# Biases as rows spread by TensorE, earlier loads, and an order from a table, in an attention and FP4 feed-forward kernel

## The chip, the cores and the metric

The kernel runs on one core of a Trainium2 chip. The core has five engines that run side by side, each with its own queue of instructions, worked off in order: TensorE (PE in the profile; its weight loads are PEld), VectorE (DVE), ScalarE (ACT), GpSimd (POOL) and SyncE (SP, which here only asks for transfers). Transfers (DMAs) are also asked for by ACT. An instruction that needs another engine's result waits at the head of its queue, and all behind it waits too.

The metric is the device time of one launch in microseconds (us). Before the change three runs gave 790.79, 791.53 and 792.86, median 791.53.

## What is computed

x has 16 batches of 512 tokens of 256 elements, in fp32. Cut to what matters:

```python
# attention, 16 heads of 16
q, k, v = x @ Wq + bq, x @ Wk + bk, x @ Wv + bv
p = exp(t - max(t))                      # per head, for t = q and t = k
q, k = p / (sum(p) + 1e-6)
attn = (q @ k.T) / (sum(q) + 1e-6)       # no softmax: it is linear
x = layernorm(x + (attn @ v) @ Wo + bo)

# feed-forward, 256 -> 704 -> 256
def fp4_linear(x, w):                    # blocks of 16 rounded to FP4 with a scale
    return fp4_quant_dequant(x) @ fp4_quant_dequant(w).T
h = silu(fp4_linear(x, w_gate)) * fp4_linear(x, w_up)
x = layernorm(x + fp4_linear(h, w_down))
```

## The kernel before

**Stages.** A batch is four tiles of 128 tokens, or two pairs of tiles; there are 32 pairs. Per batch, `project` transposes x on PE (L636) into a PSUM bank, ACT copies it out (L639), PE multiplies by Wq and Wk (L778, 128x512), DVE adds the biases (L781) and takes the maxima (L786), POOL subtracts them (L790). `features` takes exp on ACT (L801), sums, reciprocals on DVE (L803 to L814) and the scaling on POOL (L820). `key_values` sums the keys (L829), multiplies keys by x (L836), goes through Wv with its bias (L852, L853) and Wo (L864), with the copies L843, L857 and L870 between, which gives one matrix M per batch. `attend` transposes q (L636), multiplies by M (L892), adds x and b_o (from L885) and normalises (`norm`, L718 to L755), and writes the result to DRAM.

The feed-forward runs per pair. `quantise` reads the pair back (L910), rounds it to codes (`codes`, L655 to L668), and regroups the codes through DRAM (`regroup`: one write g, then four reads, L676 and L681) and the scales too (`spread_scales`: four small writes d, L699, one spreading read, L704); POOL multiplies both into xqT (L929). `gate_up` does 32 passes of PE per pair (L957; an fp32 matmul is two passes in the trace), silu and product (L962, L964), and codes, regrouping (g_h, hcT, d_h) and L1009 on POOL make hq. `down` multiplies hq by the down weights, 24 passes (L1026), normalises and writes y (L1038, asked for by ACT). The last pair, which nothing follows, transposes on PE (L977 to L995). Once, early on, the weights are rounded (`weight_scales` L509 to L534, `fp4_exact` L563 to L584) and transposed (L597, L620).

**Loads.** `load_all` asks for x of batch 0 in two halves, then on ACT's queue for Wq, Wk, Wv and on SP's for the three biases, each spread over 128 partitions by its transfer (128x256, L462). `load_x` of batch 1 asks for x and then, by `load_rest`, for w_o, b_o (spread in the same way, L466), the gate and up weights in four pieces and the down weights. x of batches 2 and 3 follows.

**What sets the order.** The code records every operation with `Plan.op(eng, us, due, fn, ins, outs, ...)`: an estimated cost in us and a due value. `Plan.order` then lists them: it goes through modelled time, always takes what can start first, and among operations of an engine that can start within 0.02 us of each other the one with the lowest due. The list fixes each engine's queue (`tc.manual_schedule`). Nothing is reordered on the chip. `LAG` is the modelled delay from an engine to another, `t_pe`, `t_dve`, `t_act`, `t_pool` give costs by size, and a transfer counts with an assumed landing time:

```python
            t, o = min(((t, o) for t, o in c if t <= first + 0.02), key=lambda x: (x[1].due, x[1].at))
```

**PSUM** has seven shared banks (tags pt, pg, pm with least and most numbers) and one that holds small tiles. Transfers go round eight semaphores: one that is issued waits for the one eight issues earlier.

Of the kernel before, what the change touches and what calls it, by code (L numbers as in the profile page):

```python
# [17 lines left out]
P = 128  # L18
# [4 lines left out]

FIRST = 2
# [3 lines left out]
LAG = 0.3  # L28
# [16 lines left out]
UNTIE = 1.0 + 2.0**-17  # L45

# [45 lines left out]
class Op:  # L92
    __slots__ = ("eng", "us", "fn", "due", "preds", "succs", "left", "bufs", "new", "start", "end", "table", "port", "name", "at")


class Plan:
# [47 lines left out]
    def order(self):  # L144
# [32 lines left out]
        def start(o, at):  # L177
            if o.port:
                at = max(at, port)
            for p in o.preds:  # L180
                at = max(at, p.end + (LAG if p.eng != o.eng else 0.0))
# [20 lines left out]
        while len(out) < len(self.ops):  # L202
# [17 lines left out]
            free[o.eng] = o.end  # L220
# [12 lines left out]
            for b in o.bufs:  # L233
                left, end = ends.get(id(b), (b.users, 0.0))
                ends[id(b)] = left - 1, max(end, o.end)
# [10 lines left out]
def t_pe(n):  # L246
    return 2 * (n / 1200.0 + 0.002)


def t_dve(n):  # L250
    return 0.15 + n / 960.0


def t_act(n):
    return 0.16 + n / 1200.0


def t_ts(n):
    return 0.15 + n / 1920.0


def t_pool(n):
    return 0.07 + n / 525.0
# [3 lines left out]
def tile_favor_fp4_block(  # L267
# [63 lines left out]
    def psum(tag, name):  # L331
        return Bank(share, tag, name)
# [57 lines left out]
    def load_x(b, due):  # L390
        x = buf([TPB, D], "x", 4, f"x_{b}")
        rows = hidden[b].rearrange("(t p) d -> p t d", p=P)
        if b:
            op("SP", 0.1, due, lambda: nc.sync.dma_start(x.tile, rows), outs=[x])
            op(f"DMA:x{b}" if b < 4 else "DMA", (0, 9.0, 16.0, 18.0, 3.5)[min(b, 4)], due, lambda: None, outs=[x])
        else:

            def halves():
                for p in range(PPB):
                    nc.sync.dma_start(x[:, 2 * p : 2 * p + 2, :], rows[:, 2 * p : 2 * p + 2, :])  # L400

            op("SP", 0.1, due, halves, outs=[x])
            for p in range(PPB):
                op(f"DMA:x{b}{p}", 4.5 + p, due, lambda: None, outs=[(x, p)])
        if b == 1:
            op("SP", 0.1, due, load_rest)
        xs[b] = x

    w_qkv = const.tile([P, DC, D3], F32, name="w_qkv")
    b_qkv = const.tile([P, D3], F32, name="b_qkv")  # L410
    w_o = const.tile([P, DC, D], F32, name="w_o")
    b_o = const.tile([P, D], F32, name="b_o")
# [32 lines left out]
    wqkv_in, wo_in = (loaded(n, t) for n, t in (("wqkv", 7.0), ("wo", 14.0)))  # L445
    NGU, NDN = NW * D // F2, DC * FF // F2
    op("DMA:wgu", 16.0, 0.0, lambda: None, outs=[(gu_b, k) for k in range(NGU)])
    op("DMA:wdn", 20.0, 0.0, lambda: None, outs=[(dn_b, k) for k in range(NDN)])
# [3 lines left out]
    def load_all():  # L452

        head = [o for o in plan.ops if o.eng == "SP"][:1]
        for o in head:
            for b in o.new:
                b.make()
            o.fn()
            o.fn = lambda: None
        for i, (w, bias) in enumerate(((Wq, bq), (Wk, bk), (Wv, bv))):  # L460
            nc.scalar.dma_start(w_qkv[:, :, i * D : (i + 1) * D], w.rearrange("(c p) n -> p c n", p=P))
            nc.sync.dma_start(b_qkv[:, i * D : (i + 1) * D], bias.partition_broadcast(P))  # L462

    def load_rest():
        nc.sync.dma_start(w_o, Wo.rearrange("(c p) n -> p c n", p=P))
        nc.sync.dma_start(b_o, bo.partition_broadcast(P))  # L466
        gu_b.make()
        dn_b.make()
        gu_raw, dn_raw = gu_rows(), dn_rows()
        for i, w in enumerate((w_gate, w_up)):  # L470
# [3 lines left out]
            nc.sync.dma_start(gu_raw[i * TR : (i + 1) * TR, 2 * NR, :], w[NR * P :])  # L474
        nc.sync.dma_start(dn_raw, w_down.rearrange("(c p) k -> p c k", p=P))

    def fill():
        make_identity(nc, ident)
        nc.gpsimd.memset(neg_half, -0.5)
# [17 lines left out]
    def weight_scales(src, src_b, n, at, name, due):  # L497
# [38 lines left out]
        op("DVE", 11 * fast + 0.0063 * nb, due, rest, ins=[pb], outs=[sc_b, *iv])  # L536
        return part, sc_b, iv

    def fp4_exact(src, src_b, scales, sc_b, iv, k, name, due):
# [14 lines left out]
        d, g, a = t_dve(F2), t_pool(F2), t_act(F2)  # L554
# [27 lines left out]
        op("DVE", t_ts(F2), due, lambda: nc.vector.tensor_scalar(c(), lower(y()), 6, None, ALU.logical_shift_left),  # L582
# [59 lines left out]
    def codes(src, xn, sq, dst, key, n, scales, at, name, due, sat=None):  # L642
# [19 lines left out]
        op("DVE", 0.27 + 0.0073 * nb, due, scale, ins=[(amax, key)], outs=[(nscale, key), (inv, key)])  # L662
# [9 lines left out]
    def regroup(src, dst, n, tag, name, due):  # L672
# [3 lines left out]
        dma(f"g{name}", 3.0, due, lambda: nc.sync.dma_start(d.tile, src.tile), ins=[src], outs=[d])  # L676
# [6 lines left out]
        dma(f"h{name}", 3.5, due, back, ins=[d], outs=[dst], issue=1.8)  # L683

    def spread_scales(nscale, G, dst, tag, name, due, holds=()):
# [8 lines left out]
        ), ins=[nscale], outs=[sT], port=True)  # L694
# [6 lines left out]
        dma(f"w{name}", 4.0, due, write, ins=[sT], outs=[d], issue=1.8)  # L701
        into, dst_b = dst

        dma(f"r{name}", 3.0 + 0.7 * G, due, lambda: nc.sync.dma_start(  # L704
# [3 lines left out]
    def norm(pr, add, dst, name, due, ins, r, junk, us=range(2)):  # L708
# [3 lines left out]
        if n == 1:  # L712
# [10 lines left out]
            op("DVE", 2 * t_dve(D) + 0.1, due, stats, ins=[(pr, key)] + ins, outs=[(r, key), st, mv])  # L723
            op("POOL", 0.7, due, lambda: nc.gpsimd.tensor_tensor(rstd.tile, mv[:, 1:2], neg_half[:, :1], ALU.pow), ins=[mv], outs=[rstd])
# [12 lines left out]
        op("DVE", n * (t_dve(D) + 0.06), due, total, ins=[(pr, key)] + ins, outs=[(r, key), rs])  # L737
# [12 lines left out]
        op("ACT", 0.35 + 0.6 * n, due, square, ins=[(r, key), rs], outs=[(dst, key), var, nm])  # L750
        op("POOL", 1.1, due, root, ins=[nm], outs=[var, rstd, nb])
# [366 lines left out]
```

## Time and profile before

| what | value |
|---|---|
| runs, median | 791.53 us |
| profiled execution, span | 792.0 us |
| PE busy | 768.6 us (97%) |
| DVE busy | 656.7 us (83%) |
| POOL busy | 455.9 us (58%) |
| ACT busy | 416.5 us (53%) |
| weights' last piece landed | 18.9 us |
| last PE pass ends | 786.8 us |

The page's chain that ended last, followed back from the last instruction, gives by engine, in shares of the span:

```profile
PE 62%; DVE 12%; DMA 8%; POOL 8%; issue 4%; ACT 4%; SPq 2%; ACTq 0%; POOLq 0%; DVEq 0%
```

Busy time counts an instruction from its start to its end. PE's passes overlap, so a pass's busy time (0.27 to 0.6 us) is more than the distance from one to the next.

### The profile page before, as it was taken

Reading aid. Unit: us, or ns where it says so; the run is one execution under the profiler, and the core shown is the slowest. Engines: PE = TensorE matmul, PEld = TensorE weight load, DVE = VectorE, ACT = ScalarE, POOL = GpSimd, SP = SyncE. Lnnn points to the kernel's source line nnn. Section 1 sums busy time; section 2 is a strip of 40 time slices with the busy share of each in tenths; the row PEclk is TensorE's granted clock in tenths of the full one; section 3 lists DMA queues with packets and bytes.
Section 4 is the critical chain, followed back from the end, with each engine's and each line's share of the span. In section 5 each row is a group of like instructions: output and inputs, shape, how many; then the busy total and the mean of one; then the engine's idle time right before and its main releaser. Section 6 shows DMA issues by size and latency. Waiting matters only on the chain.

```text
span 792.0 us, 10915 instructions
## 1 busy us (share of the span) xinstructions
PE 768.6 (97%) x3118; PEld 552.5 (70%) x3118; DVE 656.7 (83%) x1340; ACT 416.5 (53%) x893; POOL 455.9 (58%) x602
## 2 busy tenths in 40 slices
PE   7999999989998999999999999999999999999996
PEld 3567657657676777767777777777777777777774
DVE  2998999999888798697697798888878988778784
ACT  2347766868887783544545444444334444344441
POOL 5668788889887755574554435434533543543633
PEclk9999999999999999999999999999999999999998
DMA  9112411211111044404335454554554554464441
GB/s 277 45 55 86 142 53 54 82 60 62 54 53 62 30 129 133 118 37 124 100 112 138 145 171 136 152 149 134 149 154 135 145 149 140 125 179 129 136 130 41
DMA packets 104348, 89.23 MB, mean 113 GB/s; under 512 B 44512, under 2 KB 87904, under 8 KB 104288
## 3 DMA queue, kind: packets, MB, share of 16 engines
q1 hardware_dynamic: 90704, 71.49, 31.8%
q10 hardware_dynamic: 13584, 17.04, 6.0%
q8 instruction: 25, 0.41, 0.2%
q14 instruction: 35, 0.29, 0.1%
HBM read 53.28 MB, written 35.21 MB: 112 GB/s over the span
## 4 chain that ended last, share of the span: by engine, by line
PE 62%; DVE 12%; DMA 8%; POOL 8%; issue 4%; ACT 4%; SPq 2%; ACTq 0%; POOLq 0%; DVEq 0%
PE bank L957 26%; PE bank L1026 14%; PE bank L778 8%; PE bank L892 5%; PE bank L836 5%; POOL hq L1009 3%; DMA out_dram<-y 3%; DVE qk L781 2%; PE bank L636 2%; DVE mx L786 2%; DMA hcT<-g_h 2%; SPq L681 1%; POOL xqT L929 1%; DVE fs L803 1%; PE bank L852 1%
## 5 line engine op out<-in xcount | busy, mean ns | idle before, releaser
L957 PE MATMUL bank<-w_guT,xqT 128*128 128x352 f32 x1024 | 311.3, 459 | 0.0
L957 PEld LDWEIGHTS bank<-w_guT,xqT 128*128 128x128 f32 x1024 | 193.8, 190 | 100.4 <-ACT g L962 0.2
L1009 POOL TENSOR_TENSOR hq<-hcT,hq 128x384 f32<-128x384 bf16 x124 | 127.3, 1058 | 179.3 <-DMA hcT<-g_h 101.4
L1026 PE MATMUL bank<-w_dT,hq 128*128 128x256 f32 (+1 forms) x768 | 173.1, 379 | 1.1 <-DVE r L718 1.1
L1026 PEld LDWEIGHTS bank<-w_dT,hq 128*128 128x128 f32 (+1 forms) x768 | 144.9, 190 | 27.5 <-issue 1.9
L778 PE MATMUL bank<-w_qkv,xT 128*128 128x512 f32 x256 | 120.8, 602 | 3.8 <-DVE qk L781 1.9
L964 DVE TENSOR_TENSOR h<-bank,g 128x352 f32<-128x352 f32 x128 | 65.7, 515 | 50.9 <-ACT g L962 24.1
L962 ACT ACTIVATE g<-bank 128x352 f32<-128x352 f32 x128 | 57.6, 458 | 87.7 <-PE bank L957 77.8
L666 ACT ACTIVATE sq<-h,magic 128x704 f32<-128x704 uint16 x64 | 56.2, 878 | 79.2 <-DVE h L663 78.6
L820 POOL TENSOR_TENSOR qk<-qk,fr 128x512 f32<-128x512 f32 x64 | 67.0, 1073 | 20.5 <-DVE fr L814 18.9
L790 POOL TENSOR_TENSOR qk<-qk,mx 128x512 f32<-128x512 f32 x64 | 67.4, 1068 | 19.2 <-DVE mx L786 19.0
L778 PEld LDWEIGHTS bank<-w_qkv,xT 128*128 128x128 f32 x256 | 46.6, 193 | 45.4 <-issue 35.8
L755 ACT ACTIVATE y<-r,nb_d,rstd_d 128x256 f32<-128x256 f32 x60 | 32.6, 591 | 59.2 <-POOL nb_d L748 59.2
L929 POOL TENSOR_TENSOR xqT<-xcT,xs 128x256 f32<-128x256 bf16 x64 | 46.3, 740 | 27.6 <-DMA d_h<-sT_h 23.4
L836 PE MATMUL bank<-qk,x 128*128 128x256 f32 x256 | 59.7, 387 | 2.1 <-ACT qT L639 2.1
L892 PE MATMUL bank<-M,qT 128*128 128x256 f32 x256 | 59.6, 381 | 1.8 <-ACT M L870 1.8
L655 DVE TENSOR_REDUCE bank<-h 128x44 f32<-128x704 f32 x64 | 57.1, 893 | 1.6
L663 DVE SCALAR_TENSOR_TENSOR h<-h,bank 128x704 f32<-128x704 f32 x64 | 56.7, 886 | 2.1
L836 PEld LDWEIGHTS bank<-qk,x 128*128 128x128 f32 x256 | 49.5, 195 | 12.7 <-ACT qT L639 3.4
L781 DVE TENSOR_TENSOR qk<-bank,b_qkv 128x512 f32<-128x512 f32 x64 | 43.0, 681 | 18.3 <-PE bank L778 17.9
L892 PEld LDWEIGHTS bank<-M,qT 128*128 128x128 f32 x256 | 47.8, 190 | 13.2 <-ACT M L870 3.8
L885 POOL TENSOR_TENSOR xb<-x,b_o 128x512 f32<-128x512 f32 x32 | 41.0, 1285 | 22.8 <-DVE r L733 22.7
(137 smaller groups left out, 1083.3 us busy)
## 6 DMA issues: line engine op xcount, KB each, us to landing
g_h<-hw SPq DMA_DIRECT2D x31, 384.0 KB, 2.8
hcT<-g_h SPq DMA_DIRECT2D x124, 96.0 KB, 2.4
hq<-d_h SPq DMA_DIRECT2D x31, 384.0 KB, 4.1
dx<-x1n ACTq DMA_DIRECT2D x32, 256.0 KB, 2.0
x<-dx SPq DMA_DIRECT2D x32, 256.0 KB, 3.1
x<-_attn_hidden_states_dram SPq DMA_DIRECT2D x15, 512.0 KB, 3.5
out_dram<-y ACTq DMA_DIRECT2D x30, 256.0 KB, 3.3
xs<-d_x SPq DMA_DIRECT2D x32, 128.0 KB, 2.5
```

The source lines that it names most:

```text
L655: op("DVE", t_dve(n), due, lambda: nc.vector.tensor_reduce(amax[:, g], b3(src()), AX.X, ALU.max, apply_absolute_value=True), ins=[src_b], ...
L778: op("PE", t_pe(D2), due, lambda c=c, u=u, pqk=pqk: nc.tensor.matmul(pqk.tile, xT[:, 2 * c + u, :], w_qkv[:, c, :D2], start=c == 0, stop=c ...
L781: op("DVE", t_dve(D2), due, lambda t=t, pqk=pqk: nc.vector.tensor_tensor(qk[:, t, :], pqk.tile, b_qkv[:, :D2], ALU.add), ins=[pqk], outs=[ ...
L790: op("POOL", t_pool(D2), due, lambda g=g: nc.gpsimd.tensor_tensor(qk3()[:, g, :], qk3()[:, g, :], bcast(mx[:, g], HD), ALU.subtract), ins= ...
L820: nc.gpsimd.tensor_tensor(f3, f3, bcast(r[:, t * 2 * H : (t + 1) * 2 * H], HD), ALU.mult)
L836: nc.tensor.matmul(pxk[:, c * D : (c + 1) * D], x[:, t, c * P : (c + 1) * P], qk[:, t, D:], start=t == 0, stop=t == TPB - 1,)
L892: nc.tensor.matmul(pu(pa.tile)[:, u, :], qT[:, 2 * u + c, :], M[:, c, :], start=c == 0, stop=c == DC - 1,)
L957: op("PE", t_pe(F2), due + u * 0.2 * PAIR, lambda c=c, u=u, lo=lo, ps_=ps_: nc.tensor.matmul(ps_[:, :F2], xqT[:, 2 * u + c, :], w_guT[:, c ...
L962: op("ACT", t_act(F2), due, lambda g=g, pg=pg: nc.scalar.activation(g.tile, pg[:, :F2], AF.Silu), ins=[pg], outs=[g], table="silu")
L964: op("DVE", t_dve(F2), due, lambda g=g, h=h, pu_=pu_, k=k: nc.vector.tensor_tensor(h[:, k * F2 : (k + 1) * F2], pu_[:, :F2], g.tile, ALU.m ...
L1009: op("POOL", t_pool(TG * P), d, lambda u=u, c=c: nc.gpsimd.tensor_tensor(hq()[:, u, :, c, :].rearrange("p g (a t) -> p g a t", t=32), hcT. ...
L1026: op("PE", t_pe(D), due, lambda f=f, g=g, c=c, n=n, u=u: nc.tensor.matmul(pu(pd.tile)[:, u, :], hq()[:n, u, g, c, :], w_dT[:n, f, :], star ...
```

## The change

Biases: four transfers of one row each fill `b_row` [1, 1024]; two matmuls of a row of ones by half of it spread it into a bank, and two DVE copies move it into `b_all`, whose parts stand in for the old bias tiles. `load_all` asks for everything at the start, x of batches 2 and 3 included, in a new order. The planner's costs and landing times are set anew. It has a drain time for PE, an overhead per engine and a landing delay for transfers; transposes no longer reserve the port that DVE and POOL share in the model; the second half of a pair's `down` follows the first. Last, each operation's due value is replaced by a number from the table `PLACES`, two characters for each. The order of the instructions on all engines changes throughout; the number and size of the matmuls stays, but for the two added.

```diff
+AHEAD = 4
+X_AT = ((4.3, 6.0), (8.5,), (11.0,), (20.5,))
-LAG = 0.3
+LAG = 0.04
+DRAIN = 0.165
+OVER = {"DVE": 0.083, "ACT": 0.095, "POOL": 0.041}
+LANDED = 0.09
...
-                at = max(at, p.end + (LAG if p.eng != o.eng else 0.0))
+                at = max(at, p.end if p.eng == o.eng == "PE" else p.done + LAG)
...
-            free[o.eng] = o.end
+            o.done = o.end + (DRAIN if o.eng == "PE" else LANDED - LAG if o.eng.startswith("DMA") else 0.0)
+            free[o.eng] = o.end - OVER.get(o.eng, 0.0)
...
-        if b:
-            op("SP", 0.1, due, lambda: nc.sync.dma_start(x.tile, rows), outs=[x])
...
+        if b < AHEAD:
+            for p, at in enumerate(X_AT[b]):
+                op(f"DMA:x{b}{p}", at, due, lambda: None, outs=[(x, p)])
         else:
...
+            dma(f"x{b}", 7.0, due, lambda: nc.sync.dma_start(x.tile, rows), outs=[x])
...
-        for i, (w, bias) in enumerate(((Wq, bq), (Wk, bk), (Wv, bv))):
-            nc.scalar.dma_start(w_qkv[:, :, i * D : (i + 1) * D], w.rearrange("(c p) n -> p c n", p=P))
-            nc.sync.dma_start(b_qkv[:, i * D : (i + 1) * D], bias.partition_broadcast(P))
-    def load_rest():
-        nc.sync.dma_start(w_o, Wo.rearrange("(c p) n -> p c n", p=P))
-        nc.sync.dma_start(b_o, bo.partition_broadcast(P))
+        w_in = lambda q, i, w: q.dma_start(w_qkv[:, :, i * D : (i + 1) * D], w.rearrange("(c p) n -> p c n", p=P))
+        b_in = lambda q, i, v: q.dma_start(b_row[:, i * D : (i + 1) * D], v.unsqueeze(0))
+        half = lambda p: nc.sync.dma_start(xs[0][:, 2 * p : 2 * p + 2, :], rows(0)[:, 2 * p : 2 * p + 2, :])
+        half(0)
+        w_in(nc.scalar, 0, Wq)
+        b_in(nc.sync, 0, bq)
+        w_in(nc.scalar, 1, Wk)
+        b_in(nc.sync, 1, bk)
+        half(1)
+        b_in(nc.scalar, 2, bv)
+        b_in(nc.scalar, 3, bo)
+        nc.sync.dma_start(xs[1].tile, rows(1))
+        w_in(nc.sync, 2, Wv)
+        nc.sync.dma_start(xs[2].tile, rows(2))
...
+        nc.sync.dma_start(w_o, Wo.rearrange("(c p) n -> p c n", p=P))
         nc.sync.dma_start(dn_raw, w_down.rearrange("(c p) k -> p c k", p=P))
+        nc.sync.dma_start(xs[3].tile, rows(3))
...
+    def spread_biases(due):
+        for k, b in enumerate((bqk_b, bvo_b)):
+            pb = psum("pm", f"pb_{k}")
+            at = slice(k * D2, (k + 1) * D2)
+            op("PE", t_pe(D2), due, lambda pb=pb, at=at: nc.tensor.matmul(
+                pb.tile, ones, b_row[:, at], start=True, stop=True), ins=[brow_in], outs=[pb])
+            op("DVE", t_dve(D2), due, lambda pb=pb, at=at: nc.vector.tensor_copy(b_all[:, at], pb.tile),
+               ins=[pb], outs=[b])
...
-               ins=[(hc, u)], outs=[(hw, u)], port=True)
+               ins=[(hc, u)], outs=[(hw, u)])
...
-                ), ins=[(both, f"{u}{c}{int(g == TG - 1)}"), wdT_b], outs=[(pd, u)], holds=[r], name="down")
+                ), ins=[(both, f"{u}{c}{int(g == TG - 1)}"), wdT_b] + [(pd, 0)] * u, outs=[(pd, u)], holds=[r], name="down")
...
+    assert len(PLACES) == 2 * len(plan.ops)
+    for o in plan.ops:
+        hi, lo = PLACES[2 * o.at : 2 * o.at + 2]
+        o.due = DIGITS.index(hi) * len(DIGITS) + DIGITS.index(lo)
```

In the changed file the same lines stand some 96 further down: L567 is the bias matmul and L569 its copy, L605 is the old L509, L732 and L735 the old L636 and L639, L874 and L877 the old L778 and L781, L1053 the old L957, L1105 the old L1009 and L1122 the old L1026.

## Prediction

> **What bounds the kernel now.** I read the stretches first: the span cut where PE's behaviour changes. The columns are the stretch, its length, each engine's busy time with its instructions, the granted clock, DMA share and GB/s.
>
> ```profile
> core 0: us, PE busy (x) PEld busy (x) DVE busy (x) ACT busy (x) POOL busy (x), PEclk, DMA share, GB/s
> 4.26:10.12 5.86, 5.50 (x13) 3.13 (x14) 0.00 (x0) 1.17 (x2) 0.89 (x6) 1.00 0.99 262
> 10.12:22.00 11.88, 11.58 (x34) 5.42 (x33) 8.11 (x7) 2.98 (x3) 6.61 (x6) 1.00 0.95 300
> 22.00:160.00 138.00, 132.76 (x584) 92.93 (x582) 130.77 (x244) 87.21 (x188) 109.01 (x136) 1.00 0.23 74
> 160.00:260.00 100.00, 94.64 (x419) 67.86 (x420) 88.14 (x151) 77.67 (x165) 84.26 (x103) 0.98 0.16 55
> 260.00:764.00 504.00, 504.00 (x1983) 367.27 (x1983) 413.30 (x905) 239.38 (x523) 242.78 (x332) 1.00 0.45 131
> 764.00:786.80 22.80, 20.14 (x92) 15.81 (x90) 14.40 (x31) 6.77 (x15) 7.63 (x9) 1.00 0.23 70
> 786.80:792.00 5.20, 0.00 (x0) 0.00 (x0) 1.94 (x7) 0.00 (x0) 1.11 (x2) 0.60 0.15 50
> ```
>
> PE is full from 260 to 764; before 160 DVE is nearly full too (130.77 of 138). A busy PE is not yet a PE at its pace, so I took the pace from the chain of waits, where passes follow each other without a break (start, length, what):
>
> ```profile
> 214.43 6.01 PE bank L778 x14
> ...
> 272.00 9.47 PE bank L957 x32
> 281.47 1.73 PE bank L892 x8
> ...
> 286.31 0.87 PE bank L636 x8
> ...
> 300.08 5.18 PE bank L1026 x24
> ```
>
> Per pass: L778 0.429 us, L957 0.296, the 256-wide lines 0.216, the small ones 0.109. Passes of each stretch (the groups, by line) at these paces, taken from its length, leave what PE loses there: 17.74−14.5 = 3.2 us in 4.26–22; 138−130.3 = 7.7 in 22–160 (124 L778, 252 of 256 wide, 208 small); 100−90.3 = 9.7 in 160–260 (70, 180, 153 and 16 L957); −0.3 in 260–764; 22.8−18.7 = 4.1 at the end. With 4.26 before the first pass and 5.2 behind the last, 758.1 us of passes and 24.4 lost, that is the 792.0 us of the span. It lies 0.5 above the median, 791.53. **Only 24.4 us can be won by an order; PE's 758 cannot.**
>
> The early loss is DVE's. Its timeline (start, length, instruction, idle before it):
>
> ```profile
> 10.12 0.69 DVE L781 TENSOR_TENSOR qk<-bank,b_qkv 128x512 f32<-128x512 f32 x1 [10.12 <-PE bank L778]
> ...
> 19.00 3.10 DVE L509 TENSOR_REDUCE bank<-wgu 128x176 f32<-128x2816 f32 x1 [1.88 <-DMA wgu<-in_L_ffn_w_up_dram]
> 22.00 1.28 DVE L781 TENSOR_TENSOR qk<-bank,b_qkv 128x512 f32<-128x512 f32 x2
> ```
>
> **The change, part by part.** *Biases.* Two matmuls 128x512 in fp32, two passes each as L778: 4 × 0.429 = **+1.7 us**, all on PE. Two DVE copies come with them; no copy of 512 out of a bank stands on DVE before, so between L533's 0.27 (half of 0.54, 88 elements) and L781's 0.69 each; I take 0.6. The broadcasts leave the queues:
>
> ```profile
> b_qkv<-in_L_attn_bk_dram SPq DMA_DIRECT2D x1, 128.0 KB, 7.7
> d_x<-sT_x SPq DMA_DIRECT2D x128, 4.0 KB, 2.1
> ```
>
> The first L781 is put down to PE above, and the b_k broadcast landed at 2.29 + 7.7 = 10.0, so its leaving brings next to nothing there; behind the bias matmul (two cold passes, 0.85 each in the row further down) the first L877 comes at 10 to 11.8. What a one-row load takes no row shows: small pieces land in 1.8 (d_h) to 2.1, the broadcast in 7.7. The L567 of the change stands on PE behind the first four transposes and ahead of every L778, and DVE's first copy ahead of every L781, so a late row holds both engines. Asked for at about 2, it lands at 3.8 to 9.7; I take 4, nearest to the small pieces: no stall beyond x0's own landing at 4.2. The other end puts L567 at 10.0 instead of 4.7, 5.3 us more, and is a rival.
>
> *Loads.* L509 waits for wgu (11.46 + 7.42 = 18.9), and batch 1's L781 queue behind it until 22.0. By then DVE has been idle for 22.0 − 8.11 = 13.9 us. In the new order both copies and then the reduce stand there. The broadcasts' 512 KB and w_o's 256 leave the queue ahead of wgu and x2's 512 enters it, 256 KB less at 262 to 300 GB/s, so wgu lands about 0.9 earlier; but the second copy stands behind batch 0's L778 (the last L781 of it starts at 15.2 now), the first bias matmul's 1.7, x1's transposes, 8 × 0.11, and its own 0.86, which makes 18.6: I take no gain from an earlier wgu. The copies' 2 × 0.6 run in what is idle now: 13.9 − 1.2 = 12.7; if they come on top, 13.9; with the 0.9, 11.8.
>
> *Order, 22–160.* DVE sets the pace. Adding DVE's row durations up to the operation that each PE instruction needs, the tightest place in the new order is PE's 147.7th us of work, which needs 145.2 us of DVE (before: 146 and 140.4). PE's loss there is 12.7 + 145.2 + d − 147.7 − 4.26 − 3.2 (cold start) = 2.7 + d, with d DVE's idle between; the same sum before, 13.9 + 140.4 + 7.2 − 146 − 4.26 − 3.2 = 8.0, stands at the 7.7 measured (7.2 = 138 − 130.77). d lies between 0 and today's 7.2; no row tells which, and I take the middle, 3.5: 6.2 against 8.0, **−1.8**, bounds −6.2 and +3.1 with those of the idle time.
>
> *Order, 160–260.* The first gate_up pass moves from PE's 202.6th to its 221.5th us of work. Waits on one hop (a 0.61 us ACT copy or a 0.71 us L781, plus 0.26: the 0.16 by which a small pass's busy time, 0.27, exceeds its pace, and issue pieces of 0.02 to 0.05 on both sides) that other PE work doesn't cover add up to 2.3 us there in the new order and 2.2 in the old. So 7.5 of the 9.7 is not forced by single hops: it is 2.0 of granted clock (0.98 of 100 us) and longer chains, such as L836 on ACT's L639, 2.1 at once. Bounds 2.3 to 9.7; the middle is 6.0, **−3.7**.
>
> *260–764.* Lost −0.3 now: nothing to win. The chain from the last gate_up pass of a pair through codes, regrouping and L1009's first hq takes 23.0 to 28.5 (mean 25.7) in pairs 16 to 27 and lies under 29.3 us of PE, two pairs' worth (2 × (9.47 + 5.18)), before and after. **0**, with a rival below. Among the early pairs, pair 1's cover falls from 44.5 to 22.1; against chains of 17.6 to 27.7 in rows that costs 0 to 5.6. I take 0, since its first chains (pairs 0 to 3) are the short ones: 20.2, 23.1, 23.0, 17.6, mean 21.0. ACT loads its tables two times less (1.28 each), off PE's path: 0; were ACT the last to arrive, 2.6.
>
> *End.* PE waits there now (engine, line, releaser, total, times, longest):
>
> ```profile
> PE bank L991 <- DVE hd L977: 1.5, 2, 1.0
> PE bank L1026 <- DVE r L718: 1.1, 2, 0.6
> ```
>
> The single hops there are 1.5 in the old order and 1.8 in the new, of 4.1 lost; the extra 2.6 is the queueing of L991's producers. I take half of it away, **−1.1**, bounds 0 and −2.3.
>
> Sum: +1.7 − 1.8 − 3.7 + 0 − 1.1 = −4.9. 792.0 − 4.9 = 787.1, and 0.5 less for the median: **786.6 us**.
>
> Trainium skill, "TensorE: Matmul & The Clock Gate", Part 1, The HAM clock gate: the cold start is a budget of some 3.4 us of time, not a number of matmuls. The rows bear on it:
>
> ```profile
> 9.17 0.34 PEld L778 LDWEIGHTS bank<-w_qkv,xT 128*128 128x128 f32 x1 [0.52 <-issue]
> 9.82 0.19 PEld L778 LDWEIGHTS bank<-w_qkv,xT 128*128 128x128 f32 x1 [0.32 <-issue]
> ```
>
> Passes stand 0.85 apart until 9.82 and 0.43 from there, though the granted clock reads 1.00. By the rule the first bias matmul runs within a budget that is paid anyway and the two cost 1.7 together as summed; by a count of matmuls they would save 0.9. The skill's "DMA: Bandwidth & Descriptors", Specifications, speaks against the change: transfers under 512 B are read, changed and written again. A bias row of 1 KB cut into pieces falls under that, as d_x's do, which land in 2.1 us.
>
> **Rivals.** *Stalls only move.* One-hop waits that nothing covers add up to 9.7 us in the new order, 10.0 in the old, so the forced floor hardly changes, and DVE's demand before PE's 147th us grows by 145.2 − 140.4 − 1.7 = 3.1. For it: these sums. Against: 7.5 us at 160–260 is not forced by any hop. 792.0 + 1.7 − 1.1 − 0.5 = 792.1.
>
> *Slower: the hq chain outgrows its cover.* SP's order per pair puts hcT's four issues behind xcT's four, and one issue in each pair waits for y's landing:
>
> ```profile
> SPq L681 <- DMA out_dram<-y: 55.0, 17, 5.0
> ```
>
> A mean of 3.2 us, 5.0 at most. If it and xcT's issues (4 × 0.45) come ahead of hcT in every pair, the chain is 25.7 + 1.8 + 3.2 = 30.7, over 29.3 by 1.4. A microsecond over costs half a microsecond per pair, as the cover spans two: 14 pairs (16 to 29) × 0.7 = 10, so 786.6 + 10 = 797; with 5.0 each time, 809. It decides from a mean chain of 29.3. For it: pairs 17 and 27 have 1.9 and 1.1 to spare now. Against: in the new order y is asked for about 2 us earlier, and hcT met that wait 14 times of 30 before and meets it 8 times after.
>
> *Late bias row.* At 7.7 the first pass behind L567 stands at 10.0 rather than 4.7: +5.3, 791.9.
>
> **How the numbers follow.** Forecast 0.58, stalls only move 0.19, hq chain 0.14, late row 0.09. The forecast's own range: the bounds give 786.6 with −4.4 −3.7 −1.2 below (777) and +4.9 +3.7 +1.1 above (796); not all at once, so 782 to 791. For 8 in 10: 781 to 794. This kernel's runs tell 0.3% from no change, 789.2 and 793.9: faster takes 0.53 of the forecast's 0.58, 0.06 of the moved stalls and 0.02 of the late row, 0.61; slower the chain's 0.14 and 0.05 of the moved stalls and the late row, 0.19; same the rest, 0.20.
>
> **What would show it.** Right: L567 at PE before 5, the first L877 before 11.8; the loss in 22–160 near 6 and in 160–260 near 6 by the same count; 260–764 at 0; spare time before hq above 0 in each pair. Wrong: PE waiting for L567's row past 4.7; PE waits for hq from L1105; SP's wait for out_dram above 55 with hcT behind it; a loss before 260 of 17 or more.

## The result, and the profile after

The changed kernel is slower: a median of 803.86 us over five runs (801.47 to 805.06) against 791.53, a ratio of 1.0149 with a 95% interval of 1.0127 to 1.0171, or 11.8 us. Its profiled execution spans 803.3 us, 11.3 more than the one before.

The same stretches, with the columns as in the prediction (the end of the fifth is where the last pass ends):

```profile
core 0: us, PE busy (x) PEld busy (x) DVE busy (x) ACT busy (x) POOL busy (x), PEclk, DMA share, GB/s
...
4.26:22.00 17.74, 17.69 (x43) 8.36 (x44) 8.40 (x9) 2.24 (x4) 5.39 (x13) 1.00 0.82 260
22.00:160.00 138.00, 131.19 (x559) 89.97 (x559) 129.06 (x232) 82.14 (x171) 105.49 (x128) 0.99 0.20 66
160.00:260.00 100.00, 96.97 (x425) 67.88 (x424) 88.78 (x152) 76.52 (x173) 82.95 (x105) 1.00 0.16 56
260.00:764.00 504.00, 501.50 (x1977) 364.37 (x1976) 402.55 (x896) 238.01 (x516) 245.30 (x332) 1.00 0.45 131
764.00:798.10 34.10, 29.70 (x124) 21.62 (x122) 21.84 (x51) 12.31 (x27) 12.18 (x19) 1.00 0.22 68
798.10:803.30 5.20, 0.10 (x1) 0.00 (x0) 1.64 (x6) 0.00 (x0) 0.54 (x1) 0.75 0.15 50
```

What PE loses in each, counted for both profiles from the trace with the prediction's paces (a bias pass at 0.76, of which more below; the count of single records puts 22–160 before at 8.6 rather than 7.7):

| stretch | lost before | lost after | difference |
|---|---|---|---|
| 4.3 to 22 | 3.2 | 3.0 | −0.2 |
| 22 to 160 | 8.6 | 12.9 | +4.3 |
| 160 to 260 | 9.7 | 6.0 | −3.7 |
| 260 to 764 | −0.1 | 5.2 | +5.3 |
| 764 to the last pass | 4.2 | 6.5 | +2.3 |
| the added passes | | 3.05 | +3.05 |

The sum, +11.05, is the span's 11.3 within the rounding of the paces. Three places cost, and the stretch 160 to 260 gained what was forecast. The bias passes, from PE's timeline (start, length, instruction, idle before it):

```profile
4.31 1.09 PE L732 MATMUL bank<-ident,x 128*128 128x128 f32 x4 [4.31 <-DMA x<-_attn_hidden_states_dram]
5.33 2.07 PE L567 MATMUL bank<-b_row,ones 1*128 1x512 f32 x2
7.33 3.78 PE L874 MATMUL bank<-w_qkv,xT 128*128 128x512 f32 x4
...
18.09 1.12 PE L567 MATMUL bank<-b_row,ones 1*128 1x512 f32 x2
...
37.06 0.66 PE L732 MATMUL bank<-ident,qk 128*128 128x128 f32 x4 [1.05 <-POOL qk L916]
39.09 0.78 PE L732 MATMUL bank<-ident,qk 128*128 128x128 f32 x4 [1.38 <-POOL qk L916]
39.66 5.22 PE L932 MATMUL bank<-qk,x 128*128 128x256 f32 x16
```

The row of biases is there when the transposes end, so it was not late. But the first two passes take 1.0 each and the other two 0.52. The last three lines are the early loss: PE waits for POOL's scaled features of batch 0, and the 16 passes behind the waits take 5.22 us where 16 at the prediction's pace take 3.5 (the granted clock is 0.93 in 40 to 60). What POOL waited for in turn is on VectorE:

```profile
22.91 1.52 DVE L877 TENSOR_TENSOR qk<-bank,b_all 128x512 f32<-128x512 f32 x2
24.34 0.34 DVE L620 TENSOR_SCALAR bank<-bank 128x176 f32<-128x176 f32 x1
...
29.35 0.33 DVE L630 TENSOR_SCALAR wdn<-bank 128x176 f32<-128x176 f32 x1
29.59 1.21 DVE L882 TENSOR_REDUCE mx<-qk 128x64 f32<-128x1024 f32 x1
30.72 2.28 DVE L899 TENSOR_REDUCE fs<-qk 128x128 f32<-128x2048 f32 x1
```

From 24.3 to 29.6 the weights' scaling chain (L620 to L630, the old L524 to L534) stands ahead of batch 1's maximum and batch 0's sums. Before the change it ran at 37.0 to 42.3.

The late loss builds up over the whole steady part. One round, from the timelines of SP, POOL and ACT (L777 is the reading back of the codes, the old L681):

```profile
656.75 4.08 SPq L777 DMA_DIRECT2D xcT<-g_x  x4
660.87 1.86 SPq L777 DMA_DIRECT2D hcT<-g_h  x4
```

```profile
664.90 3.86 POOL L1105 TENSOR_TENSOR hq<-hcT,hq 128x384 f32<-128x384 bf16 x4 [9.61 <-DMA hcT<-g_h]
668.73 1.41 POOL L1025 TENSOR_TENSOR xqT<-xcT,xs 128x256 f32<-128x256 bf16 x2
...
671.26 0.20 POOL L844 TENSOR_TENSOR nb_d<-nm_d,rstd_d 128x2 f32<-128x2 f32 x1
```

```profile
671.49 1.09 ACT L851 ACTIVATE y<-r,nb_d,rstd_d 128x256 f32<-128x256 f32 x2 [5.00 <-POOL nb_d L844]
...
672.61 0.38 ACTq L1134 DMA_DIRECT2D out_dram<-y  x1
```

This is a closed loop. One of xcT's issues waits until the previous y has landed, as it uses the same semaphore (xcT's group takes 4.08 us; four issues of 0.45 would be 1.8). hcT is issued behind it, POOL makes hq from hcT, then xqT, then the small operations for y, ACT writes y, and y's transfer (672.61; the one before was at 656.45) is what the next xcT waits for. This round took 16.2 us. The first hq products of pairs 12 and 28, and the first passes of `down` that read them:

```profile
510.48 4.05 POOL L1105 TENSOR_TENSOR hq<-hcT,hq 128x384 f32<-128x384 bf16 x4 [5.57 <-DMA hcT<-g_h]
522.61 5.35 PE L1122 MATMUL bank<-w_dT,hq 128*128 128x256 f32 x24
...
758.59 3.87 POOL L1105 TENSOR_TENSOR hq<-hcT,hq 128x384 f32<-128x384 bf16 x4
759.93 5.69 PE L1122 MATMUL bank<-w_dT,hq 128*128 128x256 f32 x24
```

From 510.5 to 758.6 are 16 pairs, 15.5 us a pair in the mean, while PE needs 14.65. The spare time, from the end of the first hq product to the first pass of `down`, falls from 11.1 us at pair 12 to 0.3 at pair 28, and towards the end PE waits:

```profile
741.93 1.45 PE L1053 MATMUL bank<-w_guT,xqT 128*128 128x352 f32 x4 [0.76 <-DVE r L829]
...
774.20 2.63 PE L1053 MATMUL bank<-w_guT,xqT 128*128 128x352 f32 x8 [1.48 <-DVE r L829]
...
785.80 1.56 PE L1122 MATMUL bank<-w_dT,hq 128*128 128x256 f32 x6 [1.64 <-ACT hq L1091]
```

The lines name DVE and ACT, not POOL's hq. The late y holds ACT's queue, behind it stand the last pairs' codes, and with them VectorE's:

```profile
764.49 1.09 ACT L851 ACTIVATE y<-r,nb_d,rstd_d 128x256 f32<-128x256 f32 x2 [5.20 <-POOL nb_d L844]
766.95 0.85 DVE L764 TENSOR_SCALAR hcs<-sq 128x704 uint16<-128x704 uint16 x1 [4.38 <-ACT sq L762]
```

The r that PE waits for at 774.20 stands behind these codes on VectorE.

### The profile page after: what moved, and what is told of

Same layout as the page of the kernel before. It is cut to its first block, busy times and chain, and to the rows that moved or that the text cites. A ratio compares the mean times of both kernels' runs of the same rounds, so it can differ in the third digit from the quotient of the medians.

```text
span 803.3 us, 10943 instructions
## 1 busy us (share of the span) xinstructions
PE 777.1 (97%) x3122; PEld 552.2 (69%) x3122; DVE 652.3 (81%) x1342; ACT 412.5 (51%) x891; POOL 455.4 (57%) x603
## 4 chain that ended last, share of the span: by engine, by line
PE 46%; DVE 18%; DMA 11%; POOL 11%; issue 6%; ACT 5%; SPq 3%; POOLq 0%; ACTq 0%; DVEq 0%
PE bank L1053 18%; PE bank L1122 9%; PE bank L874 6%; POOL hq L1105 5%; DMA out_dram<-y 5%; PE bank L988 4%; PE bank L932 4%; DMA hcT<-g_h 2%; POOL xqT L1025 2%; SPq L777 2%; PE bank L732 2%; DVE qk L877 2%; DVE fs L899 2%; DVE bank L751 1%; DVE mx L882 1%
## 5 line engine op out<-in xcount | busy, mean ns | idle before, releaser
L1053 PE MATMUL bank<-w_guT,xqT 128*128 128x352 f32 x1024 | 313.1, 460 | 3.0 <-DVE r L829 2.4
L1053 PEld LDWEIGHTS bank<-w_guT,xqT 128*128 128x128 f32 x1024 | 193.3, 190 | 106.8 <-DVE r L829 4.3
L1105 POOL TENSOR_TENSOR hq<-hcT,hq 128x384 f32<-128x384 bf16 x124 | 126.3, 1047 | 177.8 <-DMA hcT<-g_h 146.6
L1122 PE MATMUL bank<-w_dT,hq 128*128 128x256 f32 (+1 forms) x768 | 173.9, 379 | 3.0 <-ACT hq L1091 1.6
L1122 PEld LDWEIGHTS bank<-w_dT,hq 128*128 128x128 f32 (+1 forms) x768 | 144.8, 190 | 30.9 <-ACT hq L1091 2.0
L874 PE MATMUL bank<-w_qkv,xT 128*128 128x512 f32 x256 | 122.6, 606 | 3.0 <-ACT xT L735 3.0
L916 POOL TENSOR_TENSOR qk<-qk,fr 128x512 f32<-128x512 f32 x64 | 67.9, 1084 | 29.3 <-DVE fr L910 25.2
L874 PEld LDWEIGHTS bank<-w_qkv,xT 128*128 128x128 f32 x256 | 46.9, 193 | 44.8 <-issue 33.7
L877 DVE TENSOR_TENSOR qk<-bank,b_all 128x512 f32<-128x512 f32 x64 | 43.0, 680 | 16.1 <-PE bank L874 15.8
L764 DVE TENSOR_SCALAR hcs<-sq 128x704 uint16<-128x704 uint16 x64 | 41.0, 640 | 9.6 <-ACT sq L762 9.5
```

What stands on the lines that cost most here:

```text
L874: op("PE", t_pe(D2), due, lambda c=c, u=u, pqk=pqk: nc.tensor.matmul(pqk.tile, xT[:, 2 * c + u, :], w_qkv[:, c, :D2], start=c == 0, stop=c ...
L877: op("DVE", t_dve(D2), due, lambda t=t, pqk=pqk: nc.vector.tensor_tensor(qk[:, t, :], pqk.tile, b_qkv[:, :D2], ALU.add), ins=[pqk, bqk_b], ...
L916: nc.gpsimd.tensor_tensor(f3, f3, bcast(r[:, t * 2 * H : (t + 1) * 2 * H], HD), ALU.mult)
L1053: op("PE", t_pe(F2), due + u * 0.2 * PAIR, lambda c=c, u=u, lo=lo, ps_=ps_: nc.tensor.matmul(ps_[:, :F2], xqT[:, 2 * u + c, :], w_guT[:, c ...
L1105: op("POOL", t_mix(TG * P), d, lambda u=u, c=c: nc.gpsimd.tensor_tensor(hq()[:, u, :, c, :].rearrange("p g (a t) -> p g a t", t=32), hcT.t ...
L1122: op("PE", t_pe(D), due, lambda f=f, g=g, c=c, n=n, u=u: nc.tensor.matmul(pu(pd.tile)[:, u, :], hq()[:n, u, g, c, :], w_dT[:n, f, :], star ...
```

## The experiments

All kernels compute the whole result. Where single instructions move, each engine's planned queue is edited and the rest keeps its order. Ratios are to the kernel before on the same chip (its medians there were 790.8 to 793.2), with 95% intervals; the changed kernel's is 1.0149.

### Undoing one part of the change

**The biases by broadcast again.**

```diff
-        b_in = lambda q, i, v: q.dma_start(b_row[:, i * D : (i + 1) * D], v.unsqueeze(0))
+        b_in = lambda q, i, v: q.dma_start(b_all[:, i * D : (i + 1) * D], v.partition_broadcast(P))
...
+        todo = [o for o in plan.order() if o.at not in spread]
```

> The changed kernel with the biases spread by four broadcast transfers again (asked for at the places of the one-row loads), without the two bias matmuls and their two copies; every other instruction keeps its place. Theory: the two matmuls cost PE their whole length, 3.05 us of passes (0.76 median start to start, not the 0.43 forecast), because PE's stream has no slack behind them: 3 us less than the changed kernel's 803.9, about 801, with the first matmul of the projection near 5.5 instead of 7.3. Rival: the early stretch is set by VectorE, which now waits for the weights' first reduce, so the 3 us only turn into waits further on: 803 to 804. Third: the broadcasts slow the other loads and the start gets later: 805 or more.

Measured: 800.27, ratio 1.0117 (1.0084 to 1.0150). The middle value lies 2.5 us under the changed kernel's by the ratios, but the intervals overlap, and in the profile the 3.05 us of passes are partly given back: 2.0 more are lost before 20 us, 1.5 of them waiting for Wk, which the broadcasts delay. Against that, the 16 passes behind the two waits for POOL ran at full pace in this profile, though the waits are the same:

```profile
36.19 0.66 PE L779 MATMUL bank<-ident,qk 128*128 128x128 f32 x4 [1.05 <-POOL qk L963]
38.23 0.66 PE L779 MATMUL bank<-ident,qk 128*128 128x128 f32 x4 [1.38 <-POOL qk L963]
38.72 3.62 PE L979 MATMUL bank<-qk,x 128*128 128x256 f32 x16
```

They took 5.22 us in the changed kernel. The stretch 40 to 60 there, and here:

```profile
40.00:60.00 20.00, 19.15 (x80) 13.73 (x79) 18.26 (x27) 12.29 (x23) 16.08 (x19) 0.93 0.08 27
40.00:60.00 20.00, 19.14 (x88) 13.86 (x87) 18.23 (x28) 13.79 (x27) 17.75 (x20) 1.00 0.10 33
```

These 1.6 us go with the granted clock (0.93 and 1.00), and not with the biases. Nothing firm follows for the size.

**The scaling chain back, alone.**

```diff
+            c = chains["DVE"]
+            c.remove(scaling)
+            first = next(k for k, o in enumerate(c) if o in scaling.succs)
+            c.insert(first, scaling)
```

> The changed kernel with the gate and up weights' scaling chain on VectorE (12 operations, 5.2 us) moved back from behind batch 1's first two bias adds to just ahead of its first reader, as it stood before the change; its small working tile lies in SBUF instead of a PSUM bank so that no bank is held. Theory: the loss between 20 and 60 us (7.6 us against 2.7 before the change) comes from batch 0's features standing behind that chain, so 3 to 5 us less, about 799 to 801, with the wait of 2.4 us for POOL's scaling near 37 to 39 us gone. Rival: VectorE must do the chain's 5.2 us ahead of the tightest place near 145 us of PE's work in either order, so the wait only moves to 60 to 160: 803 to 804.

Measured: 809.02, ratio 1.0225 (1.0201 to 1.0250): slower, a miss for both. The loss in 20 to 40 falls from 4.7 to 2.7 us, but the chain now stands ahead of kvT while PE has nothing else to do: one wait of 4.3 us for kvT, and ACT's work on the weights waits with it. The stretch shows a second price:

```profile
40.00:60.00 20.00, 13.69 (x47) 8.76 (x46) 18.05 (x29) 7.30 (x12) 10.44 (x11) 0.74 0.08 27
```

The granted clock is 0.74 there, and 10.0 us are lost, some 5 of them by the clock (0.26 of 20). The place was wrong for an order of PE's that has no other work at 45 us; what the chain costs is not read from this run.

**The chain later, with everything around it planned anew.**

```diff
+    held = op("DMA:hold", 32, 0.0, lambda: None, outs=[hold])
...
-        op("DVE", 2.0 + 0.015 * nb, due, rest, ins=[pb], outs=[sc_b, *iv])
+        op("DVE", 2.0 + 0.015 * nb, due, rest, ins=[pb] + [hold] * (name == "g"), outs=[sc_b, *iv])
```

> The changed kernel, planned with one line more: the weights' scaling chain on VectorE may not start before 32 us of the model's time. The order up to about 300 us is planned anew around that (the chain stands behind batch 2's bias adds and the sums of keys, and ACT's and POOL's work on the weights behind it too, which the earlier try left in place); the steady part is the same. Theory: the early loss is VectorE's: at 24.3 us the planner took the scaling chain, 5.2 us, ahead of the maxima that batch 0's and 1's features need, since an operation that follows its own producer counts 0.12 us later than one that doesn't and ties reach 0.02 only; put later, the loss in 20 to 60 falls from 7.6 to 3 to 5 us: 799 to 801. Rival: VectorE has to do the same work before PE's 147th us in any order, the loss comes back by 160: 803 to 805.

Measured: 818.44, ratio 1.0352 (1.0332 to 1.0372). The stretches 22–60, 60–160 and 160–260 of this kernel:

```profile
22.00:60.00 38.00, 36.35 (x148) 23.06 (x147) 37.13 (x60) 17.69 (x31) 25.12 (x29) 1.00 0.08 28
60.00:160.00 100.00, 91.69 (x399) 64.01 (x398) 89.32 (x171) 63.87 (x133) 79.42 (x97) 0.98 0.26 81
160.00:260.00 100.00, 88.03 (x383) 62.82 (x382) 77.20 (x142) 72.97 (x167) 79.88 (x102) 0.95 0.15 53
```

The early loss went as expected: in 20 to 60 it is 2.9 us instead of 7.6. But the later stretches lose 13 and 18 us, against 5 and 6 in the changed kernel: PE waits 3.5 and 7.3 us for POOL's scaling there. That the table's numbers fit one order only would explain it, but no run shows that. The place of the chain is confirmed for its own stretch only.

**y written from SP's queue.**

```diff
+            for i in range(8, 26):
+                o, x = by[name[f"y{i}_0"]], by[name[f"rx{i + 5}"]]
+                chains["ACT"].remove(o)
+                o.fn.__defaults__ = o.fn.__defaults__[:1] + (nc.sync,)
+                chains["SP"].insert(chains["SP"].index(x) + 1, o)
```

> The changed kernel with the writes of y of pairs 8 to 25 asked for by SP, behind xs of the same round, instead of by ACT; all else keeps its place. Theory: in the steady stage each round closes a loop: y's landing frees SP's queue at xcT (a shared semaphore), behind which stand hcT, hq, and by POOL's order y of the next pair; it takes 15.5 us where PE's pair takes 14.65, so the chain to hq grows by 0.8 a pair until PE waits from pair 26 on. Without it SP's wait for out_dram (42.8 us in 500 to 764) falls below 10, the chain stays near 20 us, the loss after 700 us falls from 9.3 to about 4: 798 to 799. Rival: the chain grows for another reason (VectorE's or ACT's order, hcT behind xcT), then the wait goes and the chain still grows: 803 to 804; or SP's queue is itself longer than PE's pair and the extra issue makes it worse: 805.

Measured: 797.04, ratio 1.0076 (1.0052 to 1.0100), 5.8 us better than the changed kernel by the ratios, with intervals apart. SP's queue in the same place of this kernel:

```profile
666.56 1.95 SPq L824 DMA_DIRECT2D xcT<-g_x  x4
668.55 1.85 SPq L824 DMA_DIRECT2D hcT<-g_h  x4
670.45 0.54 SPq L847 DMA_DIRECT2D xs<-d_x  x1
671.08 0.54 SPq L1181 DMA_DIRECT2D out_dram<-y  x1
```

xcT takes 1.95 us, without a wait. SP's wait for out_dram in 500 to 764, in the changed kernel and here (total, times, longest):

```profile
SPq L777 <- DMA out_dram<-y: 42.8, 17, 4.5
SPq L824 <- DMA out_dram<-y: 1.0, 1, 1.0
```

The chain to hq stays at 18 to 21.7 us, its spare time at 8 to 12, and after 700 us only 1.7 are lost instead of 9.3.

**The same loop cut on POOL.** rstd and nb for y stand behind the second hq product instead of behind all of hq and xqT.

```diff
+            for i in range(8, 27):
+                root = by[at[f"y{i}_0"] - 3]
...
+                if c[j - 1].at in hqs:
+                    c.insert(j - 2, c.pop(k))
```

> The changed kernel with the three small operations on POOL that make rstd and nb for y (1.1 us) moved from behind all four hq products and both xqT products to behind the second hq product, for pairs 8 to 26. It cuts the same loop at another place than the write by SP did: y is ready some 3.5 us earlier in each round. Theory: SP's wait for out_dram falls below 15 us in 500 to 764, the chain to hq stays short and the loss after 700 falls to 2 to 4: 797 to 799. Rival (the write's own issue on ACT or its shared semaphore matter, not when y is ready): 802 to 804.

Measured: 797.08, ratio 1.0043 (1.0027 to 1.0058). SP's waits in 500 to 764 (total, times, longest):

```profile
SPq L824 <- DMA out_dram<-y: 23.6, 13, 5.2
```

Down from 42.8, but not below the 15 expected (3.7 more wait on L847); the spare time falls to 2.0 at pair 19 and rises again, and 1.6 us are lost after 700. Two cuts at different places of the loop take away the same late loss. Here ACT still asks for y, so it is when y is ready that counted.

**xcT and hcT in the old order.**

```diff
+                h, x = c.index(by[name[f"hh{i}"]]), c.index(by[name[f"hx{i + 3}"]])
+                if h == x + 1:
+                    c[x], c[h] = c[h], c[x]
```

> The changed kernel with hcT's four transfers ahead of xcT's four on SP again for pairs 8 to 27, all else in place. If hcT's place behind xcT is what lengthened the round (15.5 us in the changed kernel, 15.2 before the change), the chain is some 1 us shorter each round, the wait for out_dram falls on hcT again, and the loss after 700 us falls from 9.3 towards 4 to 6: 799 to 801. If the loop through y's landing is what counts and the order within it little, 802 to 804.

Measured: 802.29, ratio 1.0134 (1.0095 to 1.0174), not apart from the changed kernel's. In its profile the spare time still falls, from 11.3 us at pair 12 to 0.2 at pair 28. The swap is tried from the other side below.

**Biases and y together.**

```diff
+        b_in = lambda q, i, v: q.dma_start(b_all[:, i * D : (i + 1) * D], v.partition_broadcast(P))
...
+                o.fn.__defaults__ = o.fn.__defaults__[:1] + (nc.sync,)
+                chains["SP"].insert(chains["SP"].index(x) + 1, o)
```

> Both of the edits that gained: the biases by broadcast transfers and y of pairs 8 to 25 asked for by SP. Theory: the bias passes lie in the first 20 us, the loop through y's landing after 480 us, so the gains of 3.6 and 6.8 us add: 803.9 - 10.4 = 793.5, with 1.7 us lost after 700. Rival: an earlier feed-forward stage gives the chain to hq less to hide behind, or the early gain is lost between 60 and 160: 795 to 797.

Measured: 796.28, ratio 1.0073 (1.0051 to 1.0094), the same as with y alone (1.0076). The profile loses 1.9 more before 20 than the changed kernel, as with the biases alone, and 9.1 us against 7.6 in 20 to 60, which together is what the passes gave. But the second part is mostly the clock again. One wait and the 16 passes behind both, here:

```profile
36.62 0.66 PE L779 MATMUL bank<-ident,qk 128*128 128x128 f32 x4 [1.50 <-POOL qk L963]
...
39.56 6.04 PE L979 MATMUL bank<-qk,x 128*128 128x256 f32 x16
```

The passes take 6.04 us, 5.22 in the changed kernel and 3.62 with the biases alone; the wait is 1.50 instead of 1.05. Before 20 us, then, the broadcasts cost some 2 of the 3 us that the passes take, and what is left, about 1 us, is less than the runs can tell.

**Without the table.**

```diff
-    assert len(PLACES) == 2 * len(plan.ops)
-    for o in plan.ops:
-        hi, lo = PLACES[2 * o.at : 2 * o.at + 2]
-        o.due = DIGITS.index(hi) * len(DIGITS) + DIGITS.index(lo)
```

> The changed kernel without the table of places: dues as before the change, with the new costs, loads and bias matmuls, so a new order everywhere. If the table is what costs (the order it gives between 300 and 760 us and at the end), this is nearer to the kernel before: 795 to 800. If the new costs and the two matmuls are (the scaling chain stands early here too, and y's write on ACT shares its semaphore with SP's reads in every order), it is as slow or slower: 803 to 812.

Measured: 816.07, ratio 1.0308 (1.0276 to 1.0339). The table alone is not what costs: without it, the new costs, loads and biases with the old dues are 24 us slower than before, and with it 12. The old dues were made for the old costs, so this says nothing about the costs by themselves.

### Doing one part alone, in the kernel before

**Biases as rows, nothing else.**

```diff
-            nc.sync.dma_start(b_qkv[:, i * D : (i + 1) * D], bias.partition_broadcast(P))
+            (nc.sync if i < 2 else nc.scalar).dma_start(b_row[:, i * D : (i + 1) * D], bias.unsqueeze(0))
...
+                nc.tensor.matmul(bank, ones, b_row[:, half], start=True, stop=True)
+                nc.vector.tensor_copy(b_all[:, half], bank)
```

> The kernel before the change with the biases as rows: four one-row loads instead of four broadcasts, and two matmuls and two copies at the places they have in the changed kernel (the bank of the small tiles serves as theirs); nothing else moves. Forecast of the prediction: +1.7 us of passes. By the changed kernel's trace: 3.05 us of passes (0.76 each), less nothing: about 794. Rival, from the two undo runs (3.6 us won alone, 0.8 together with the other edit): the early stretch waits for VectorE and the weights' load, so most of it is hidden and the two copies (1.4 us of VectorE) are what counts: 791 to 793. If the earlier landing of the other loads gives it back: 790 or less.

Measured: 794.78, ratio 1.0024 (1.0008 to 1.0040): +1.9 us, between 0.6 and 3.2.

```profile
6.46 2.04 PE L1086 MATMUL bank<-b_row,ones 1*128 1x512 f32 x2 [1.13 <-DMA b_row<-in_L_attn_bk_dram]
...
18.96 1.12 PE L1086 MATMUL bank<-b_row,ones 1*128 1x512 f32 x2
```

The passes last as long as in the changed kernel, 1.0 and 0.5, and the row came 1.1 us late here, but in 22 to 60 PE loses less than before, 0.3 us of idle instead of 1.9 by its busy time (37.71 and 36.07 of 38). What makes up for it is not shown.

**The scaling chain early, nothing else.**

```diff
+            red = c.index(next(p for p in scaling.preds if p.eng == "DVE"))
+            c.insert(red + 3, c.pop(k))
```

> The kernel before the change with the gate and up weights' scaling chain on VectorE (12 operations, 5.2 us) moved up to right behind batch 1's first two bias adds, where the changed kernel has it; nothing else moves. Theory: batch 0's features come 5 us later, PE runs out of work at 25 to 45 us, the loss in 20 to 60 goes from 2.7 to 6 to 8 us and isn't made up later: 794 to 797. Rival: VectorE does the chain in any case before the stretch is over, so the loss comes back by 160: 791 to 792.5.

Measured: 797.08, ratio 1.0045 (1.0029 to 1.0061): +3.6 us. PE's waits in 20 to 60 of this kernel:

```profile
PE bank L683 <- POOL qk L867: 5.3, 2, 5.0
```

The same wait as in the changed kernel, for POOL's scaled features, 5.3 us here. In this profile, of the slowest of its runs (799.25), the loss in 20 to 60 rises from 2.7 to 8.7, some 3.4 of it by the clock (0.91 in 22 to 60); about 2 come back by 260, and at the end 1.8 more are lost than before.

**xcT ahead of hcT, nothing else.**

```diff
+                h, x = c.index(by[name[f"hh{i}"]]), c.index(by[name[f"hx{i + 3}"]])
+                if x == h + 1:
+                    c[x], c[h] = c[h], c[x]
```

> The kernel before the change with xcT's four transfers ahead of hcT's four on SP for pairs 8 to 27 (where they stood next to each other), as in the changed kernel. Theory of the loop: the wait for y's landing then falls on xcT and hcT's four issues come behind it, up to 1.4 us more per round; the spare time before hq, which falls from 8.7 us at pair 12 to 1.1 at pair 27, runs out some pairs earlier and PE waits from then on: 794 to 798, with a loss after 600 us of 4 to 8 instead of 3.6. If the order within a round is not what matters (undoing it in the changed kernel gave 1.6 us, not clear of noise): 791 to 792.5.

Measured: 797.00, ratio 1.0046 (1.0030 to 1.0062): +3.6 us. The spare time before `down` runs down to 0.2 at pair 17 and to 0.1 at pairs 26 and 27; 8.9 us are lost after 580, where 3.9 were.

**y from SP, nothing else.** The edit is the one made above in the changed kernel.

```diff
+                o.fn.__defaults__ = o.fn.__defaults__[:1] + (nc.sync,)
+                chains["SP"].insert(chains["SP"].index(x) + 1, o)
```

> The kernel before the change, with y of pairs 8 to 25 asked for by SP behind xs. Theory: there too the chain to hq grows by 0.5 us a pair (spare 8.7 us at pair 12, 1.1 at pair 27), it only just fits, so in the steady stage nothing is won, and at the end, where 3.6 us are lost after 760, the last pairs start with their codes ready earlier: 789 to 790.5. If the tail is set by the last pair's own work alone: 791.5. If an SP queue that issues one transfer more per pair is the limit: 792 or more.

Measured: 791.15, ratio 1.0000 (0.9990 to 1.0011). The spare time now stays at 8.4 to 11.9 in pairs 12 to 27, where it fell from 8.7 to 1.1. So the old order has the loop too, but its chain just fits, and cutting it wins nothing.

## Why the prediction was wrong

Forecast 786.6, measured 803.86; the rival with the hq chain, at 797, had been given 0.14.

*What held.* The biases: 1.7 was the sum, 1.9 (0.6 to 3.2) is what they cost alone in the old order, though by other numbers: a pass takes 1.0 or 0.52 instead of 0.43, and less is lost behind them. Nor did the first two passes fall into a cold start that is paid anyway: before, the passes reach full pace at 9.82, and here the four behind them, 7.33 to 10.90, still take 0.85 to 1.0 each. The pieces under 512 B that spoke against the rows don't show: in the first 30 us there are 228 packets under 512 B with the rows, and 288 with the four broadcasts. The row landed in time (L567 starts at 5.33, no wait), so that rival fell. The first L877, forecast at 10 to 11.8, is at 11.15. In 160 to 260, 6.0 us of loss were forecast and 6.0 measured, and here luck helped: 6.0 was the middle of 2.3 to 9.7, taken for want of a row. Part of the gain is the granted clock, 0.98 before and 1.00 after; three kernels that keep the old order there (y from SP, rows, chain early) read 1.00 with nearly the same waits, so this part is not the new order's.

*260–764, "0, with a rival below": the step that failed most, as the late part of the end hangs on it.* 5.2 us are lost instead of none, and 6.5 at the end instead of 3.0. The working set a mean chain of 25.7 us against a cover of 29.3 and asked how far one round had to grow. The rows it came from were more than scatter: they run from 23.0 at pair 16 to 28.5 at pair 27, and the spare time from 6.6 to 1.1, with pair 17 (1.9) out of line. That is a trend, 0.5 us a pair, of a loop that is longer than PE's pair (15.2 us against 14.65). It is a trend of the mean only: with xcT and hcT swapped in the old kernel, the spare time stands at 1.6 to 1.7 in pairs 21 to 25. The old order survived because the pairs ended before the spare did. The question was the loop's period, and how many pairs were left. In the changed kernel it is 15.5, so 0.8 to 0.9 us a pair, and the spare ends at pair 26. Cutting the loop on SP brings 5.8 us, on POOL 8.4 (by the ratios). The rival named hcT behind xcT: alone in the old order that costs 3.6, but undoing it in the changed kernel wins nothing clear. Its argument against, that y is asked for earlier, didn't count, as y itself is in the loop. Its price, 10, was near the 5.8 to 8.4, by a sum of single rounds that is not what happened. Its sign, SP's wait for out_dram above 55, did not show either: the wait fell to 42.8.

*Order, 22–160, "d lies between 0 and today's 7.2", 3.5 taken.* d is 138 − 129.06 = 8.9, over the upper bound. The sum 2.7 + d gives 11.6; 12.9 was lost where 6.2 was forecast, some 1.6 of it by the clock behind the two waits. The bound was no bound: nothing keeps a new order from idling VectorE more. The prefix sum looked only at how much VectorE has to do by PE's 147th us, and so missed the order within it: the scaling chain ahead of the maxima starves PE at 24 to 40, and later, with PE behind, VectorE waits for PE (15.39 busy of 20 in 60 to 80, 16.42 before). Done alone in the old order, the early chain costs 3.6 us.

*End, −1.1.* It became +2.3. The saving was to come from the queueing of L991's producers; the old waits for hd, 1.5, are gone, but two waits of 1.5 for r and 1.6 for the last pair's hq stand in their place, behind the late y.

The three parts done alone, 1.9 + 3.6 + 3.6, and the gain of 3.7 at 160 to 260 leave some 6 of the 11.8 us to the rest of the order, if they add, which no run shows. The loop cut whole (5.8 to 8.4 instead of the 3.6 for the swap) takes 2 to 5 of it. What lengthens the loop besides the swap stays open, and so does how the early 4.3 us divide between the chain and the clock: both runs that put the chain back in the changed kernel were slower. Why the planner took the chain early is read from the code alone: an operation that follows its own producer on an engine counts 0.12 us later than one that doesn't (`OVER` and `LAG`), and dues decide only within 0.02. No run tests it.

No kernel here beats the one before.

## What to carry to other kernels

A chain that is hidden in every round is not safe: list its spare time round by round, and if it falls steadily, find the loop that is longer than the bounding engine's round and compare the loop's period with that engine's, not the chain's mean with its cover. Transfers that share a semaphore close such loops between queues that have nothing to do with each other; where y is asked for, or behind what it is computed, was worth 5.8 to 8.4 us here, and the four bias passes alone 1.9. And a sum of work up to a place says what an order can reach, not what it does: put the first few operations of each engine in time, one after the other.

## What the hardware showed unexpectedly

A pass with a single row (1x512) took 0.52 us from start to start where one of 128 rows took 0.43, and 1.0 against 0.85 in the first ones. After a PE wait of 4.3 to 5.0 us the granted clock of the stretch around it fell: 0.74 in 40 to 60 where the scaling chain held kvT, 0.91 in 22 to 60 where it stood early in the old kernel. In the changed kernel 0.93 in 40 to 60 followed two waits of 1.05 and 1.38 us with one short group of passes between; with the biases by broadcast the same two waits left it at 1.00. So two executions with the same waits can differ by the 1.6 us that the 16 passes behind them lost. The Trainium skill, "TensorE: Matmul & The Clock Gate", Part 1, The HAM clock gate, has the clock fall after an idle window of some 3.4 us; the two long waits agree with it, the two short ones, 2.4 us together, don't by themselves. The one-row transfers that the first matmul needs landed within 3.6 us of being asked for in the changed kernel (1.70 to 5.33), and 1.1 us later than PE wanted them in the old order of loads.
